# A graph layer: part of one gathered tile in every 11th group comes by identity products on TensorE, and the prologue is laid out anew

## The chip, the cores and the metric

The kernel runs on one core of a Trainium2 chip. Its time is the device time of one execution in microseconds. The kernel before takes 1875.99 us, the median of three runs (1874.75 to 1878.42). The trace shown here comes from one more execution, which took 1872.44 us and whose instructions span 1870.6 us.

The engines are named as the profile names them: PE is TensorE's products and PEld its weight loads, DVE is VectorE, ACT is ScalarE, POOL is GpSimd and SP is SyncE, which only issues transfers here.

## The reference

The layer has 12500 nodes with 64 features and 212500 edges with 32 features. The edges are sorted by destination. All numbers are f32.

```python
msg_in = jnp.concatenate([nodes[row], nodes[col], edge_features], axis=-1)
messages = relu(msg_in @ mW1 + mb1) @ mW2 + mb2
aggregated = jax.ops.segment_sum(messages, col, num_segments=nodes.shape[0])
upd_in = jnp.concatenate([nodes, aggregated], axis=-1)
out = relu(upd_in @ uW1 + ub1) @ uW2 + ub2
result = _layernorm(nodes + out, axis=-1)
```

`row` is the source of an edge and `col` its destination. The costly part is `nodes[row]`: 212500 rows of 64 features, read in no order.

## The kernel before

**Groups and steps.** The edges are cut into 554 groups of 384, each of three tiles of 128. Because the edges are sorted, the destinations of a group lie in a window of 32 nodes. One step of the main loop handles three groups at once on TensorE: it turns group k (`turn`, L372), forms the hidden layer of group k - 2 (`hidden`, L399) and sums group k - 4 into its window (`sums`, L425). Every step is one unbroken run of matmuls; its first instruction waits for all that the three parts need, and its last one releases what follows.

**Where source features come from.** For most tiles POOL issues an indirect transfer (`gather`, L164 to L175, issue at L167) that brings 128 rows into a slot of a ring of 20 groups. It works 16 groups ahead of the steps; the slot of group g is free when group g - 20 has been turned. TensorE then turns the rows into columns (L378, one product with an identity for each tile), so that features lie along the partitions, and ACT copies the result from PSUM to SBUF (L389). The first tile of the groups in `COPIED`, 181 of them, has no gather: the node features lie in SBUF as columns (`own_xc`, 64 partitions by 12500), and DVE and ACT copy one column of 4 bytes for each edge straight into its place (`fetch`, L553 to L569). Each step copies 44 columns: 20 on DVE (L565), 24 on ACT (L567). The addresses come from a table of sources (`src_copied`): SP loads a piece for eight steps, DVE turns it into addresses (L531), and before each part a register load on the copying engine brings up to 12 of them into registers (L546). From step 18 (`BEGIN`) to step 543 the steps copy columns; the last 10 (`SHORT`) do not.

**The other parts of a step.** DVE writes the one-hot of the destinations in the window (L366), which lies beside the gathered rows. The hidden layer is a product of 128 turned rows (64 features, 32 one-hot, 32 edge features) with 128x128 weights in which the 32 middle rows are the window's projected nodes (L404); DVE applies the relu (L415). The sums multiply the hidden layer as weights with the one-hot (L431). The one-hot is repeated `TIMES` = 4 times as the moving operand, which gives 128 columns of which 32 are used. Every fourth step counts the edges of each node (L442). Every 23 steps or so a chunk of 512 nodes is finished and updated (L474 to L516).

**The prologue.** SP loads tables and the eight weight tiles (L217, L218). ACT fills the sums with zeros (L267) and the ones row of `own_xc` and the zeros beside it (L206, in a small and a large piece). The projections of the nodes by their destination weights (`projected`, L335) go through two buffers to a table in DRAM (L343, L344), from which the windows are read (L358). At step 8 the checks on the edges' order and the combined weights are made (L281 to L310).

## Time and profile before

| what | value |
|---|---|
| median of three runs | 1875.99 us |
| the profiled execution | 1872.44 us |
| its span | 1870.6 us |
| busy: PE, PEld | 1302.0 us, 1139.3 us |
| busy: DVE, ACT, POOL | 1452.9 us, 1558.7 us, 1400.1 us |
| mean granted TensorE clock | 0.952 |

Busy times of PE and PEld overlap each other, and a product's end is modelled; the distance between the starts of two instructions says more of their cost than their durations. A row of a group gives, behind its name, the shapes, the count, the busy time in us, the mean duration in ns, and the idle time of the engine just before, with what ended it. For TensorE the shape is `128*96 128x128`: rows and columns of the weights, then partitions and columns of the operand that moves (in a weight load's row, the weights again). In a row of the timeline the first two numbers are the start and the time covered, and `x6` says that six neighbours of one kind were put together. A row of stretches gives their bounds, their length, then the busy time and count of PE, PEld, DVE, ACT and POOL, the granted clock as a share, the share of the DMA engines and GB/s.

### The profile page before, as it was taken

The page shows a single profiled execution, that of the slowest core. Times are in us where ns is not written, and L with a number is a line of the kernel's source. Part 1 is how long each engine was busy: PE and PEld are TensorE (multiplying, and loading weights), DVE is VectorE, ACT ScalarE, POOL GpSimd, SP SyncE. Part 2 cuts the span into 40 slices and gives each one's busy share as a digit, 9 for nine tenths or more (in the row PEclk, how much of TensorE's full clock was granted, in tenths as well). Part 3 has the DMA queues.
Part 4 walks back from the last instruction along what each step waited for, and adds up shares of the span by engine and source line. Part 5 has one row for each costly group of instructions (what it writes and reads, how often), then busy time and mean ns, then how long its engine had stood idle before and what let it go on. Part 6 is the DMA issues. An engine that isn't in the chain of part 4 may idle for free. (4 is left out here: it accounts for less than half of the span.)

```text
span 1870.6 us, 55967 instructions
## 1 busy us (share of the span) xinstructions
PE 1302.0 (70%) x9839; PEld 1139.3 (61%) x9839; DVE 1452.9 (78%) x13141; ACT 1558.7 (83%) x13374; POOL 1400.1 (75%) x1488
## 2 busy tenths in 40 slices
PE   1777777677767667677676776776767767667676
PEld 0676666666666556566665666665656656556665
DVE  1338888899897888877887878888878888888773
ACT  5249999999998888888888888888888888888871
POOL 7777777777777777777777777777777777777774
PEclk9889999999999998998999998999998999999999
DMA  4543222222222222222222222222222222222221
GB/s 93 138 123 75 54 54 54 51 54 53 52 54 48 50 52 49 50 49 45 54 52 47 52 46 54 48 51 48 53 46 53 45 54 51 48 53 48 50 49 26
DMA packets 112796, 104.10 MB, mean 56 GB/s; under 512 B 51586, under 2 KB 82960, under 8 KB 112432
## 3 DMA queue, kind: packets, MB, share of 16 engines
q0 software_dynamic: 47392, 48.60, 14.8%
q1 hardware_dynamic: 64196, 51.35, 10.0%
q14 instruction: 280, 2.29, 0.4%
q8 instruction: 84, 1.38, 0.3%
q10 hardware_dynamic: 844, 0.48, 0.1%
HBM read 90.61 MB, written 9.62 MB: 54 GB/s over the span
## 5 line engine op out<-in xcount | busy, mean ns | idle before, releaser
L167 POOL DMA_INDIRECT own_s<-in_x,src_sb x1481 | 1399.4, 945 | 452.5 <-issue 342.9
L567 ACT ACTIVATE own_st<-own_xc 64x4 uint8 x12560 | 1265.6, 192 | 60.2 <-issue 52.2
L565 DVE COPY own_st<-own_xc 64x4 uint8 x10480 | 884.5, 190 | 17.3 <-issue 9.2
L378 PE MATMUL own_ps<-own_ident,own_s 128*96 128x128 f32 x1661 | 294.1, 288 | 488.7 <-DMA own_s<-in_x,src_sb 164.0
L378 PEld LDWEIGHTS own_ps<-own_ident,own_s 128*96 128x96 f32 x1661 | 169.1, 131 | 593.5 <-issue 291.0
L431 PE MATMUL own_ps<-own_s,own_h 128*128 128x128 f32 x3322 | 490.3, 287 | 1.2 <-DVE own_h L415 0.6
L404 PE MATMUL own_ps<-own_wm,own_st 128*128 128x128 f32 x3322 | 485.5, 285 | 0.0
L415 DVE TENSOR_SCALAR own_h<-own_ps 128x384 f32<-128x384 f32 x553 | 302.1, 547 | 185.5 <-PE own_ps L442 84.7
L431 PEld LDWEIGHTS own_ps<-own_s,own_h 128*128 128x128 f32 x3322 | 443.3, 203 | 2.3 <-DVE own_h L415 1.2
L404 PEld LDWEIGHTS own_ps<-own_wm,own_st 128*128 128x128 f32 x3322 | 437.8, 201 | 1.8 <-issue 1.2
L389 ACT ACTIVATE own_st<-own_ps 96x384 f32<-96x384 f32 (+2 forms) x734 | 294.2, 401 | 167.5 <-PE own_ps L442 81.6
L458 DVE TENSOR_TENSOR own_agg<-own_ps,own_agg 128x32 f32 x554 | 105.8, 191 | 170.6 <-DVE own_h L415 90.4
L366 DVE TENSOR_TENSOR own_s<-iota,dlc 128x96 f32<-128x96 f32 x554 | 136.2, 247 | 0.3 <-issue 0.2
L442 PE MATMUL own_ps<-own_s,own_one 128*1 128x128 f32 x834 | 120.6, 283 | 0.0
L463 DVE TENSOR_TENSOR own_xc<-own_ps,own_xc 1x32 f32 x554 | 101.9, 184 | 18.5 <-DVE own_xc L463 1.8
L442 PEld LDWEIGHTS own_ps<-own_s,own_one 128*1 128x1 f32 x834 | 60.2, 85 | 35.7 <-issue 3.6
L340 PE MATMUL u_ps<-w1b,own_xc 65*128 65x128 f32 x196 | 33.4, 323 | 58.1 <-ACT t L343 38.8
L340 PEld LDWEIGHTS u_ps<-w1b,own_xc 65*128 65x128 f32 x196 | 29.1, 227 | 62.3 <-ACT t L343 42.1
L343 ACT ACTIVATE t<-u_ps 128x512 f32<-128x512 f32 (+1 forms) x25 | 14.7, 588 | 58.2 <-DMA by_dst<-t 37.9
L487 PE MATMUL u_ps<-same,own_xc 65*128 65x64 f32 (+1 forms) x196 | 37.0, 271 | 1.5 <-ACT u L480 1.4
L489 PE MATMUL u_ps<-u,u 128*128 128x64 f32 (+1 forms) x196 | 38.0, 276 | 0.0
L487 PEld LDWEIGHTS u_ps<-same,own_xc 65*128 65x128 f32 (+1 forms) x196 | 29.7, 191 | 2.3 <-ACT u L480 2.2
(62 smaller groups left out, 257.1 us busy)
## 6 DMA issues: line engine op xcount, KB each, us to landing
own_st<-in_efT SPq DMA_DIRECT2D x138, 192.0 KB
own_s<-in_x,src_sb POOLq DMA_INDIRECT x1481
own_wm<-by_dst SPq DMA_DIRECT2D x554, 16.0 KB
by_dst<-t SPq DMA_DIRECT2D x24, 256.0 KB
out<-o SPq DMA_DIRECT2D x24, 128.0 KB
own_xc<-in_xT SPq DMA_DIRECT2D x12, 179.2 KB
index<-in_src_copied SPq DMA_DIRECT2D x65, 1.4 KB
dlc_i<-in_dst_cols SPq DMA_DIRECT2D x1, 831.0 KB
```

The lines of the kernel that those rows point to most:

```text
L167: nc.gpsimd.indirect_dma_start(out=s[:p, j, :D], out_offset=None, in_=x[:, :], in_offset=bass.IndirectOffsetOnAxis(ap=src_sb[:p, g * TG + ...
L366: places_by[g] = nc.vector.tensor_tensor(own.s[g % RING][:, :, D:], iota.unsqueeze(1).to_broadcast([P, TG, W]), dlc[:, g * TG : (g + 1) * ...
L378: nc.tensor.transpose(xt[:, j * P : j * P + p], s[:p, j, :], ident[:p, :p])
L389: after(nc.scalar.activation(t[r, c : c + n][:, m], xt[r, m], AF.Copy), step))
L404: nc.tensor.matmul(pre[:p, j, :], t[:, c + j * P : c + j * P + p], wm[g % NW], start=True, stop=True)
L415: relu_by[g] = [nc.vector.tensor_scalar(h, pre, 0.0, None, ALU.max)]
L431: did.append(nc.tensor.matmul(sg, h[:p, j, :], s[:p, j, D:].unsqueeze(1).to_broadcast([p, TIMES, W]), start=j == 0, stop=j == len(sizes) - 1))
L442: did.append(nc.tensor.matmul(at_ps[:, : len(whole)], own.one, own.ring[:, first_s : first_s + len(whole), j, D:], start=j == 0, stop=j == ...
L458: did = [after(nc.vector.tensor_tensor(agg[:, at], sg[:, 0, :], agg[:, at], ALU.add), step)]
L463: did.append(after(nc.vector.tensor_tensor(count, counted, count, ALU.add), step))
L565: by[engine] = nc.vector.tensor_copy(o, x_at)
L567: by[engine] = nc.scalar.activation(o, x_at, AF.Copy)
```

## The change

It has two parts.

**Products instead of gathers.** In 47 groups (29, 40, and so on to 535, `BY_PE`) the third tile loses its gather. Its 128 source columns are brought by TensorE: behind the matmuls of each step, `side_fetch` issues up to 12 matmuls with the same weights, the first 64 rows and 96 columns of the identity, and one moving column each, a column of `own_xc` at an address from a register. The result goes straight to the place in PSUM where the turned tile would stand; rows 64 to 95 come out as zeros. The 128 columns take 11 steps. In front of each step's matmuls `side_columns` loads the step's addresses into TensorE's registers. In the step that turns such a group, the third tile's turning is replaced by a product of its one-hot with the identity, which fills rows 64 to 95. The table of sources has 56 entries for each step instead of 44. The one-hot of the sums is repeated twice instead of four times (`TIMES`).

**The prologue.** The zeros of the sums are written by DVE in 16 pieces, two ahead of the first projections and one in each of the first 14 steps. The ones row and the zeros below it, now with the row of counts, are written by ACT in a piece for each of the first 16 steps, behind the early piece. Half of the weight tiles' loads, most of the destination table, and the update weights go behind the first windows. The projections' rows have four buffers instead of two.

```diff
-TIMES = 4
+TIMES = 2
+PCOLS = 12
+PERIOD = 11
+EACH = COLS + PCOLS
+SIDE = 512 - P
+BY_PE = [g for g in range(BEGIN + PERIOD, G - SHORT, PERIOD)]
...
-            for j, p in enumerate(tiles_of(g)) if j or g not in columned
+            for j, p in enumerate(tiles_of(g))
+            if (j or g not in columned) and (j < TG - 1 or g not in by_pe)
...
-    rowp = ctx.enter_context(tc.tile_pool(name="rows", bufs=2))
+    rowp = ctx.enter_context(tc.tile_pool(name="rows", bufs=4))
...
-    nc.scalar.activation(agg.rearrange("p (a b) -> p a b", a=P),
-                         zero.unsqueeze(1).to_broadcast([P, P, NP // P]), AF.Copy)
-    rest(NEAR_NODES, NP)
...
         nc.sync.dma_start(xc[:D, slice(*nodes)], a["xT"][:, slice(*nodes)])
+        rest(nodes[0], nodes[1] if k < BITS - 1 else NP)
+
+    def zeroed(k):
+
+        n0, n1 = (NP * i // BITS for i in (k, k + 1))
+        nc.vector.memset(agg[:, n0:n1], 0.0)
...
+        xt = ps[0][: D + W, 512 - GE :] if g in by_pe else ps[0][: D + W, :GE]
+        did = []
+        for j, p in enumerate(tiles_of(g)):
+            cols = slice(j * P, j * P + p)
+            if j == TG - 1 and g in by_pe:
+                did.append(nc.tensor.matmul(xt[D:, cols], s[:, j, D:], ident,
+                                            start=True, stop=True))
+            else:
+                did.append(nc.tensor.transpose(xt[:, cols], s[:p, j, :], ident[:p, :p]))
...
+    def side_columns(k):
+
+        if k < BEGIN:
+            return None
+        n, m = divmod(k - BEGIN, PERIOD)
+        c0, c1 = m * PCOLS, min(P, (m + 1) * PCOLS)
+        if n >= len(BY_PE) or c0 >= c1:
+            return None
+        return BY_PE[n], c0, loaded(k, COLS, c1 - c0, ET.PE)
+
+    def side_fetch(k, work):
+
+        if work is None:
+            return
+        g, c0, v = work
+        for c, at in enumerate(v, SIDE + c0):
+            i = nc.tensor.matmul(own.ps[g % 2][0][: D + W, c : c + 1], ident[:D, : D + W],
+                                 xc_bytes[:D, bass.ds(at - own.at, 4)].bitcast(F32),
+                                 start=True, stop=True)
+            tc.no_tile_sem_insts.add(i.ins.name)
+            tc.add_to_no_dep_group("quiet", i.ins)
+            kept[:] = [i.ins]
...
-    inputs(0)
-    inputs(1)
     for g in range(LEAD):
         onehot(g)
+    placed()
     places(0)
+    weights(SB)
+    inputs(0)
+    for i in (0, 1):
+        zeroed(i)
     projected(0)
     projected(1)
     for g in range(SB):
         window(g)
+    nc.sync.dma_start(dlc_i[:, near:], a["dst_cols"][:, near:])
+    update_weights()
+    weights(NW)
+    inputs(1)
+    relative(NEAR_GROUPS, G)
...
+            side = side_columns(k)
             between.append(lambda: registers(k, 0))
             step((turn, k), *([(hidden, k - 2)] if k > 1 else []),
                  *([(sums, k - 4)] if k > 3 else []))
+            side_fetch(k, side)
```

More of the change, by code (lines that the diff above doesn't have):

```diff
@@ L44 @@
 NEAR_NODES = 1024
+NEAR_GROUPS = 16
 BITS = 16
@@ L139, in ordered @@
     efs_by, hidden_by, counted_by = {}, {}, {}
-    columned = set(COPIED)
+    columned, by_pe = set(COPIED), set(BY_PE)
     def after(first, *others):
-        tc.declare_no_dep(first.ins, group="quiet", reason="waits for the last of a step")
+        keep = kept if first.ins.engine == ET.PE else []
+        tc.declare_no_dep(first.ins, group="quiet", keep=keep,
+                          reason="waits for the last of a step")
         for i in others:
@@ L189, in ordered @@
     nc.vector.memset(eps, EPS)
-    zero = const.tile([P, NP // P], F32, name="zero")
-    nc.vector.memset(zero, 0.0)
     nc.vector.tensor_copy(ident, ident_t)
@@ L544, in registers @@
                 return
[L545 to L551 removed]
+            held[part] = engine, c0, loaded(k, offset, count, engine)
     def fetch(*parts):
```

116 lines of the change are left out of this document (65 added, 51 removed).

## The prediction

> **What bounds the kernel now.** I read the page first (busy shares, slices, groups), then POOL's waits, then three stretches with TensorE's counts, and last TensorE's timeline, because the change moves work from POOL to TensorE.
>
> ```profile
> span 1870.6 us, 55967 instructions
> PE 1302.0 (70%) x9839; PEld 1139.3 (61%) x9839; DVE 1452.9 (78%) x13141; ACT 1558.7 (83%) x13374; POOL 1400.1 (75%) x1488
> L167 POOL DMA_INDIRECT own_s<-in_x,src_sb x1481 | 1399.4, 945 | 452.5 <-issue 342.9
> L567 ACT ACTIVATE own_st<-own_xc 64x4 uint8 x12560 | 1265.6, 192 | 60.2 <-issue 52.2
> ```
> ```profile
> L167 POOL DMA_INDIRECT own_s<-in_x,src_sb x1481: 901/944/1667, 3.0 to 1852.5; - x186
> ```
> ```profile
> POOL own_s L167 <- issue: 342.9, 1125, 0.3
> POOL own_s L167 <- DMA own_s<-in_x,src_sb: 85.3, 280, 0.3
> POOL own_s L167 <- PE own_ps L431: 19.2, 63, 0.3
> ```
>
> By busy share ACT (83%) looks like the bound and POOL (75%) does not. POOL's waits say otherwise: the idle time in front of a gather is never longer than 0.3 us (last column), whoever is named as its releaser. The gathers run from 3.0 to 1852.5 us, so one takes (1852.5 - 3.0) / 1480 = 1.2497 us, 0.945 busy and 0.30 of issue, and POOL stands still for nothing else. POOL bounds the whole span: 1481 gathers in a row, then 18 us for the last groups.
>
> ```profile
> 0.00:121.69 121.69, 61.67 (x412) 56.98 (x413) 32.71 (x126) 41.61 (x40) 90.84 (x102) 0.90 0.50 120
> 121.69:1792.75 1671.06, 1187.78 (x9035) 1038.14 (x9034) 1379.88 (x12736) 1488.63 (x13127) 1263.23 (x1339) 0.96 0.24 52
> 1792.75:1870.60 77.85, 52.59 (x394) 44.20 (x394) 40.36 (x281) 28.48 (x209) 46.06 (x49) 0.93 0.19 39
> ```
> ```profile
> 121.69:1792.75 1671.06, 273.07 (x1551) 155.50 (x1551) 0.96 0.24 52
> ```
>
> The columns are PE, PEld, DVE, ACT, POOL, then the granted clock. The middle stretch runs from step 18 to step 534; the row in the second fence counts only its turning (L378), three per step, so it holds 1551 / 3 = 517 steps of 3.23 us. These are the 517 steps that the change gives new TensorE work. In front of it TensorE is late: the gathers of group 18 are issued by 3.0 + 57 x 1.25 = 74 us, its step runs at 121.7.
>
> **What a pass on TensorE costs.** A matmul in f32 is two passes, each a weight load and a product; a turning is one. Busy times overlap here, so I go by starts in the timeline.
>
> ```profile
> 86.91 0.97 PEld L340 LDWEIGHTS u_ps<-w1b,own_xc 65*128 65x128 f32 x8
> 87.80 0.35 PEld L378 LDWEIGHTS own_ps<-own_ident,own_s 128*96 128x96 f32 x3
> 88.13 0.75 PEld L404 LDWEIGHTS own_ps<-own_wm,own_st 128*128 128x128 f32 x6
> 88.80 0.75 PEld L431 LDWEIGHTS own_ps<-own_s,own_h 128*128 128x128 f32 x6
> 89.47 0.97 PEld L340 LDWEIGHTS u_ps<-w1b,own_xc 65*128 65x128 f32 x8
> ```
> ```profile
> 802.95 1.02 PE L474 MATMUL u_ps<-own_agg,wc 128*128 128x512 f32 x2
> 803.81 1.02 PE L475 MATMUL u_ps<-own_xc,ux 97*128 97x512 f32 x2
> 809.40 0.39 PE L489 MATMUL u_ps<-u,u 128*128 128x64 f32 x2
> 809.63 0.39 PE L487 MATMUL u_ps<-same,own_xc 65*128 65x64 f32 x2
> 809.85 0.39 PE L489 MATMUL u_ps<-u,u 128*128 128x64 f32 x2
> ```
> ```profile
> 1859.51 0.20 PEld L442 LDWEIGHTS own_ps<-own_s,own_one 128*1 128x1 f32 x6
> 1859.65 0.26 PEld L448 LDWEIGHTS own_ps<-own_s,own_one 128*1 128x1 f32 x4
> 1862.07 0.27 PEld L489 LDWEIGHTS u_ps<-u,u 128*106 128x106 f32 x2
> 1862.25 0.35 PEld L487 LDWEIGHTS u_ps<-same,own_xc 65*106 65x106 f32 x2
> ```
> ```profile
> L306 PE MATMUL u_ps<-valid,ones x4: 163/164/164, 78.1 to 80.0; 128*1 128x1 f32 x4
> L442 PEld LDWEIGHTS own_ps<-own_s,own_one 128*1 128x1 f32 x834 | 60.2, 85 | 35.7 <-issue 3.6
> 1003.45 0.28 PEld L378 LDWEIGHTS own_ps<-own_ident,own_s 128*96 128x96 f32 x3 [1.76 <-ACT own_st L567]
> ```
>
> With 128 weight columns and 128 moving columns six passes take 0.67 us, 0.112 each (88.13 to 88.80). With 64 moving columns a pass still takes 0.111 (809.40 to 809.85, four passes): the weight load sets it. With 512 moving columns it is 0.43 (802.95 to 803.81, two), and the weight load vanishes in it. With 106 weight columns it is 0.09 (1862.07 to 1862.25, two); with one weight column and 32 moving ones 0.02 to 0.03 (1859.51 to 1859.65, six). So a pass lasts as long as the longer of its weight load and its product, and the load goes by its columns, about 0.85 to 0.88 ns for each. L306 has four records for two matmuls with one moving column: two passes there too. L442 uses one and the same weights in every matmul and yet loads them every time (834 loads, as many as its products on the page's list).
>
> **The change, part by part.** *Gathers.* The 47 groups lose one gather each: 47 x 1.2497 = 58.7 us of POOL's row. That is the whole gain if POOL stays the bound: 1870.6 - 58.7 = 1811.9.
>
> *Column products.* 47 tiles of 128 columns are 6016 matmuls, two passes each: 12032 passes, 24 in a full step. Each loads the 64x96 identity for a single moving column. No such pass is in the trace. From above: 0.09 us (106 columns). From below: 0.03 (one column). I take 96 / 128 x 0.112 = 0.084, next to the 106 column row, since the load goes by columns. That is 12032 x 0.084 = 1011 us, 2.0 us in a full step. TensorE has not that much room. Its own passes in the middle stretch are 9034 x 0.112 = 1012, and 92 of them, the 512 column ones of 23 chunks, cost 0.32 more: 29; together 1041. The room is 1671 - 1041 = 630 us, against 1011.
>
> *The third tile's one-hot* in those 47 groups becomes a product of two passes with 128 moving columns instead of one turning: about 0.11 x 47 = 5 us.
>
> *Register loads on TensorE*, one of up to 12 values per step:
>
> ```profile
> L546 ACTq TENSOR_LOAD <-index x1047: 549/782/1358, 123.6 to 1814.8; - x175
> ```
>
> On ACT one takes 0.78 us in the sequencer. On TensorE it is queued behind the 24 passes of the step before, and the whole step that follows is queued behind it. I take nothing for it, covered by those 2.0 us of passes already issued; uncovered it is 517 x 0.782 = 404 us.
>
> *TIMES 4 to 2* halves the moving columns of the sums to 64. By the 809 rows a pass stays at 0.111: nothing, and no loss.
>
> *Prologue.*
>
> ```profile
> L343 ACT ACTIVATE t<-u_ps 128x512 f32<-128x512 f32 (+1 forms) x25 | 14.7, 588 | 58.2 <-DMA by_dst<-t 37.9 <-PE u_ps L340 16.0 <-PE own_ps L431 4.3
> L206 ACT ACTIVATE own_xc<-own_ident 32x1024 f32<-32x1024 f32 (+1 forms) x2 | 10.8, 5424 | 0.0
> L267 ACT ACTIVATE own_agg<-zero 128x12544 f32<-128x12544 f32 x1 | 10.7, 10657 | 9.9 <-DMA own_wm<-in_mW 9.9
> L191 DVE MEMSET zero<- 128x98 f32 x1 | 0.1, 140 | 0.0
> 10.86 0.54 SPq L217 DMA_DIRECT2D own_wm<-in_mW  x1
> 22.08 0.88 SPq L316 DMA_DIRECT2D own_st<-in_efT  x2
> ```
>
> Two fills leave ACT's queue ahead of the first table copy: 10.7 + 9.8 = 20.5 us. The zeros come back on DVE as 16 pieces of 784 columns, at most 8 x 0.14 = 1.1 us each, 18 us, in a stretch where DVE works 32.7 of 121.7 us; the ones come back on ACT in 16 pieces of about 0.8 us, where it works 41.6. On SP half of the 16 weight loads (10.86 to 22.08) go behind the first features. The seven update weights on ACT's queue and the larger part of the destination table on SP go behind the first windows; they are first used at steps 8 and 10, so I take nothing. Nothing new stands ahead of POOL's gathers. Four row buffers instead of two can take some of the 37.9 us for which the copies wait for their own writes; I count 13. While POOL is the bound all this is worth nothing, since POOL starts at 3.0 either way. Once TensorE is, it counts: step 18 moves from 121.7 to 121.7 - 20.5 - 13 = 88, between 77 (its gathers) and 122 (no help).
>
> *Tail.* 77.9 us are now 49 gathers long. With POOL up to 20 groups ahead I estimate 70, between 58 and 78.
>
> *Sum.* 88 + (1041 + 5 + 1011 = 2057) + 70 = 2215 us of span, 2217 with the 1.8 that the profiled execution (1872.44) has around its span; the median of the runs shown, 1875.99, is 0.2% above that execution: 2220. A middle step becomes 2057 / 517 = 3.98 us instead of 3.23, and POOL, with 1434 gathers, waits for the ring. ACT and DVE, 1488.6 and 1379.9 us busy in those 1671, keep their work and get slack.
>
> **The rivals.** *A, POOL stays the bound: faster.* One mechanism: the identity's load costs next to nothing. For it: the three 96 column loads of a turning (1003.45) stand in 0.28 us all told, and a one column weight pass costs 0.03. Against it: those rows turn data in one pass or load a single column; 106 columns of plain f32 took 0.09. It decides at (1671 + 34 + 8 - 1046) / 12032 = 0.055 us per pass; at or under (1671 - 59 - 1046) / 12032 = 0.047 the time is 1811.9 + 1.8, with the 0.2% 1817. [...] *A', in between:* a pass midway between 0.03 and 0.09 gives 2220 - 12032 x 0.024 = 1931.
>
> *B, loads and products do not overlap, or the register load is exposed.* A pass of 0.084 + 0.028 adds 337 us: 2557; an uncovered register load adds 404: 2624. For it: no product here has so short a stream to hide a load in, and no register load stands in TensorE's queue now. Against it: the 512 column rows swallow their loads whole. [...]
>
> *C, the clock falls, or register-addressed products run at ACT's pace.*
>
> ```profile
> 60.00:80.00 20.00, 8.00 (x60) 6.28 (x59) 7.21 (x22) 2.54 (x5) 15.10 (x16) 0.76 0.57 140
> 1500.00:1520.00 20.00, 12.52 (x102) 10.93 (x102) 15.52 (x142) 16.37 (x146) 15.15 (x16) 1.00 0.28 58
> ```
>
> The granted clock was 0.76 where PE worked 8 of 20 us, 1.00 with 12.5 of 20. One-column products may count as little work: 0.76 instead of 0.96 in the middle makes 2057 into 2598, the time 2760. ACT's register-addressed copies take 1265.6 / 12560 = 0.101; in series with the load a pass is 0.185: 3435.
>
> *D, the change does not relieve POOL* cannot be: the gathers leave the list.
>
> **Chances and range.** TensorE bound at 0.080 to 0.092 a pass 0.64, its own range 2150 to 2360; A 0.11; A' 0.03 (0.01 of it within 0.2%); B 0.16; C 0.06. The range, 2060 to 2750, reaches from below TensorE's own range to over both prices of B and leaves out A, A' and C, 0.20. A measurement can tell about 0.2%: faster 0.11, same 0.01, slower 0.88.
>
> **What would show it.** Right: POOL with 1434 gathers and idle times of many us that TensorE's turning ends; PE and PEld each with about 21,900 records; column passes 0.08 to 0.09 us apart; steps of about 4.0 us in the middle; ACT's share well under 83%; the first turning before 37.9 us. Wrong: gathers still 1.25 us apart (A), passes 0.11 or more apart or gaps of 0.8 us at each step's head (B), a granted clock under 0.9 in the middle (C).

## The result, and the profile after

The changed kernel takes 3932.02 us, the median of four runs (3911.54 to 3978.18); the kernel before took 1875.78 us beside it (1874.75 to 1878.42). The ratio is 2.092, with a 95% interval of 2.083 to 2.101; it leaves out the longest of the four runs, which showed a lower clock (0.589) than the others (0.597 to 0.599). The forecast said slower, and named TensorE as the new bound; both came true. Its time, 2220 us, and its range, 2060 to 2750 us, did not. The profiled execution took 3926.39 us.

These are lines of the page after: the span, the engines' busy time, the granted clock in 40 slices and the costliest groups. In the changed kernel a gather is L177, a column product L625, a turning L413, ACT's copy of the turned tiles L422, a hidden product L437 and a sum L464.

```profile
span 3924.6 us, 86426 instructions
PE 3688.3 (94%) x21918; PEld 3436.5 (88%) x21918; DVE 1497.3 (38%) x13158; ACT 1634.9 (42%) x13388; POOL 1359.9 (35%) x1441
PEclk8556565665665655565555555665655555555567
L177 POOL DMA_INDIRECT own_s<-in_x,src_sb x1434 | 1359.1, 948 | 2483.0 <-PE own_ps L464 1438.3
L625 PEld LDWEIGHTS own_ps<-own_xc,own_ident 64*96 64x96 f32 x12032 | 1665.2, 238 | 263.6 <-ACT own_st L422 192.1
L625 PE MATMUL own_ps<-own_xc,own_ident 64*96 x12032 | 1709.3, 271 | 140.7 <-ACT own_st L422 137.5
L437 PE MATMUL own_ps<-own_wm,own_st 128*128 128x128 f32 x3322 | 754.4, 392 | 0.0
```

The kernel before had these two rows for the clock and for the hidden products:

```profile
PEclk9889999999999998998999998999998999999999
L404 PE MATMUL own_ps<-own_wm,own_st 128*128 128x128 f32 x3322 | 485.5, 285 | 0.0
```

POOL has its 1434 gathers and now waits 2483 us, mostly for TensorE (1438.3 us for its sums, 731.3 for its counts). TensorE is busy 94% of the span. But the clock row is new: it read 8 or 9 in every slice before, and reads 5 or 6 in all but the first and the last here. The hidden products carry no change at all in the diff and their records grew from 285 ns to 392 ns. The same three stages as in the forecast, with the columns PE, PEld, DVE, ACT, POOL and the clock:

```profile
0.00:89.00 89.00, 57.62 (x412) 53.42 (x412) 43.88 (x143) 34.31 (x54) 66.53 (x75) 0.92 0.54 141
89.00:3851.90 3762.90, 3575.95 (x21112) 3337.26 (x21112) 1416.64 (x12768) 1574.74 (x13150) 1293.37 (x1367) 0.58 0.10 24
3851.90:3924.60 72.70, 54.71 (x396) 45.77 (x395) 36.81 (x249) 25.87 (x186) 0.00 (x0) 0.88 0.05 14
```

The prologue (89 us) and the tail (72.7) are where the forecast put them (88 and 70). Everything that is missing is in the middle: 3763 us in place of 2057, with a clock of 0.58. The timeline of TensorE shows the same step twice, once at full clock (492.14) and once at half (497.39); the first number is the start, the second the time covered.

```profile
492.14 2.19 PE L625 MATMUL own_ps<-own_xc,own_ident 64*96 x24
494.27 0.53 PE L413 MATMUL own_ps<-own_ident,own_s 128*96 128x128 f32 x3
494.63 0.83 PE L437 MATMUL own_ps<-own_wm,own_st 128*128 128x128 f32 x6
...
497.39 4.00 PE L625 MATMUL own_ps<-own_xc,own_ident 64*96 x24 [0.75 <-ACT own_st L422]
501.31 0.88 PE L413 MATMUL own_ps<-own_ident,own_s 128*96 128x128 f32 x3
501.98 1.49 PE L437 MATMUL own_ps<-own_wm,own_st 128*128 128x128 f32 x6
503.26 1.38 PE L464 MATMUL own_ps<-own_s,own_h 128*128 128x64 f32 x6
```

At full clock 24 column passes take 494.27 - 492.14 = 2.13 us. The starts inside such a run are 0.085 us apart (median of some 3800), so the 0.084 of the forecast was right. At half clock they are 0.160 apart (median of some 7700), and a 128 column pass takes 0.213 in place of 0.112.

In both traces the granted clock has two values only, 1.0 and 0.5 (82 records before, 288 after), and its changes lie whole multiples of 3.413 us apart. The records of half clock add up to 181 us before and 3168 us after. A window is, from here on, a stretch of that length on the grid of these changes. What goes with the clock shows in consecutive windows of after: first all products that overlap them (the count in brackets), then the column products alone; the clock is the column behind.

```profile
485.12:488.53 3.41, 3.24 (x16) 0.50 0.00 1
488.53:491.95 3.42, 3.42 (x33) 1.00 0.09 18
491.95:495.36 3.41, 3.41 (x37) 1.00 0.33 88
495.36:498.77 3.41, 2.66 (x16) 0.50 0.16 38
498.77:502.19 3.42, 3.42 (x21) 0.50 0.06 16
```
```profile
485.12:488.53 3.41, 0.01 (x1) 0.50 0.00 1
488.53:491.95 3.42, 1.51 (x16) 1.00 0.09 18
491.95:495.36 3.41, 2.19 (x24) 1.00 0.33 88
495.36:498.77 3.41, 1.38 (x9) 0.50 0.16 38
498.77:502.19 3.42, 2.62 (x17) 0.50 0.06 16
```

The window at 491.95 is busy from end to end with 37 products, and the next one is at half clock; the one at 485.12 holds only 16, and the next one is at full clock. The difference is in the second fence: 24 of the 37 are column products, only 1 of the 16 is. Counted over the whole traces, by the starts of a step's own passes in each window (turning, hidden, sums, counts and update; a pass of 512 columns as four, a column product as none), this is the share of windows that are followed by one at full clock, with the number of windows:

| own passes in the window | under 11 | 11 or 12 | 13 or 14 | 15 to 17 | 18 and more |
|---|---|---|---|---|---|
| before | 0 (24) | 0.27 (30) | 0.87 (38) | 1.00 (160) | 0.99 (280) |
| after | 0 (628) | 0.07 (116) | 0.20 (162) | 0.68 (188) | 0.98 (46) |
| after with `TIMES = 4` | 0 (556) | 0.29 (150) | 0.87 (132) | 0.93 (176) | 0.95 (39) |

So a window with 13 or 14 own passes was followed by full clock just as often (0.87) before, where there are no column products, as after with `TIMES = 4`, where a full step has 24 of their passes; with fewer than 11 own passes none was. With `TIMES = 2` a third of the own passes stream 64 columns, and 13 or 14 gave 0.20, 15 to 17 gave 0.68. This also shows why the clock comes back so seldom. A step has some 18 own passes. At full clock its 24 column passes take 2.1 us of a window, which leaves room for some 12 own ones. At half clock they take 24 x 0.160 = 3.84 us, more than a whole window, and a window without any of them has room for 3.41 / 0.213 = 16 own passes.

### The profile page after: what moved, and what is told of

Its sections match the earlier page's. It is cut to its first block, busy times and chain, and to the rows that moved or that the text cites. A ratio compares the mean times of both kernels' runs of the same rounds, so it can differ in the third digit from the quotient of the medians.

```text
span 3924.6 us, 86426 instructions
## 1 busy us (share of the span) xinstructions
PE 3688.3 (94%) x21918; PEld 3436.5 (88%) x21918; DVE 1497.3 (38%) x13158; ACT 1634.9 (42%) x13388; POOL 1359.9 (35%) x1441
## 4 chain that ended last, share of the span: by engine, by line
issue 45%; PE 27%; POOL 23%; DMA 2%; ACT 1%; DVE 0%; SPq 0%; ACTq 0%; POOLq 0%; DVEq 0%
POOL own_s L177 23%; PE own_ps L625 12%; PE own_ps L437 5%; PE own_ps L464 5%; PE own_ps L413 3%; PE own_ps L475 1%; DMA own_s<-in_x,src_sb 1%; ACT own_st L422 1%; PE u_ps L369 1%; PE u_ps L520 0%; PE u_ps L522 0%; ACT own_st L605 0%; PE u_ps L507 0%; DMA by_dst<-t 0%; DMA own_xc<-in_xT 0%
## 5 line engine op out<-in xcount | busy, mean ns | idle before, releaser
L177 POOL DMA_INDIRECT own_s<-in_x,src_sb x1434 | 1359.1, 948 | 2483.0 <-PE own_ps L464 1438.3
L625 PEld LDWEIGHTS own_ps<-own_xc,own_ident 64*96 64x96 f32 x12032 | 1665.2, 238 | 263.6 <-ACT own_st L422 192.1
L625 PE MATMUL own_ps<-own_xc,own_ident 64*96 x12032 | 1709.3, 271 | 140.7 <-ACT own_st L422 137.5
L422 ACT ACTIVATE own_st<-own_ps 96x384 f32<-96x384 f32 (+2 forms) x734 | 298.7, 407 | 2041.8 <-PE own_ps L464 1308.1
L437 PE MATMUL own_ps<-own_wm,own_st 128*128 128x128 f32 x3322 | 754.4, 392 | 0.0
L464 PEld LDWEIGHTS own_ps<-own_s,own_h 128*128 128x128 f32 x3322 | 718.2, 311 | 6.3 <-DVE own_h L448 4.7
L464 PE MATMUL own_ps<-own_s,own_h 128*128 128x64 f32 x3322 | 716.0, 383 | 4.1 <-DVE own_h L448 3.1
L437 PEld LDWEIGHTS own_ps<-own_wm,own_st 128*128 128x128 f32 x3322 | 695.7, 302 | 19.8 <-issue 15.7
L413 PE MATMUL own_ps<-own_ident,own_s 128*96 128x128 f32 x1614 | 426.6, 393 | 53.1 <-DMA own_s<-in_x,src_sb 26.5
L413 PEld LDWEIGHTS own_ps<-own_ident,own_s 128*96 128x96 f32 x1614 | 216.0, 169 | 69.3 <-issue 35.8
L475 PE MATMUL own_ps<-own_s,own_one 128*1 128x128 f32 x834 | 174.1, 369 | 0.0
```

What stands on the lines that cost most here:

```text
L177: nc.gpsimd.indirect_dma_start(out=s[:p, j, :D], out_offset=None, in_=x[:, :], in_offset=bass.IndirectOffsetOnAxis(ap=src_sb[:p, g * TG + ...
L413: did.append(nc.tensor.transpose(xt[:, cols], s[:p, j, :], ident[:p, :p]))
L422: after(nc.scalar.activation(t[r, c : c + n][:, m], xt[r, m], AF.Copy), step))
L437: nc.tensor.matmul(pre[:p, j, :], t[:, c + j * P : c + j * P + p], wm[g % NW], start=True, stop=True)
L464: did.append(nc.tensor.matmul(sg, h[:p, j, :], s[:p, j, D:].unsqueeze(1).to_broadcast([p, TIMES, W]), start=j == 0, stop=j == len(sizes) - 1))
L475: did.append(nc.tensor.matmul(at_ps[:, : len(whole)], own.one, own.ring[:, first_s : first_s + len(whole), j, D:], start=j == 0, stop=j == ...
```

## The experiments

On three of the chips used here the kernel before itself takes about 2435 us (last section); each run is set against the kernel before on its own chip.

The theory after the two traces was the one just told: one-column products do not count as work for the clock. Its rivals were the other parts of the change (narrow sums, prologue), the register loads that sit between the steps, and the wait of the products for ACT's copy.

**First: is it the clock, the prologue, or the narrower sums?** One chip, kernel before 2434.52 us.

```diff
 e1_times4
-TIMES = 2
+TIMES = 4
```

> The changed kernel with TIMES back at 4 and nothing else. Where the granted clock was 0.5 for 3168 of 3925 us, the theories differ in what lowers it. Theory S (a stretch of products with one moving column streams almost nothing through the array, so the clock is cut): the sums' six passes stream 0.107 instead of 0.053 us each, which helps a little; mean clock 0.62 to 0.75, time 3100 to 3800. Theory T (the sums' halved moving columns lower it): clock over 0.9, time near 2340, which is 3925 less half of the 3168 us at half clock. Theory G (gaps in front of each step, from the register load on TensorE, lower it): as measured, about 3930.

3700.39 us in one run, clock 0.68. The wide sums bring some windows back (third row of the table), not most of them.

```diff
 e2_no_products
-BY_PE = [g for g in range(BEGIN + PERIOD, G - SHORT, PERIOD)]
+BY_PE = []
...
```

> The changed kernel without the column products: all 181 + 47 groups' third tiles are gathered as before, 1481 gathers; the new prologue and TIMES = 2 stay. Theories S and G: clock near 0.95 as in the kernel before, POOL bounds, and the time is that of before within 0.3% (1872 to 1880), since the prologue lies beside POOL's row. Theory T: the sums' passes at half the stream lower the clock under 0.8; a step's 15 passes at half clock take about 3.2 us, so TensorE becomes a second bound and the time goes over 1950.

2458.11 us, a ratio of 1.009 (1.005 to 1.012). Without the products the loss is gone but for a remainder; the times that were expected (1872 to 1880) were for a chip on which the kernel before takes 1876. The next run says where the remainder may be from.

```diff
 e4_before_times2 (the kernel before)
-TIMES = 4
+TIMES = 2
```

> The kernel before with TIMES = 2 and nothing else. Theories S and G: POOL bounds as before; the array streams about 1.45 instead of 1.77 us of a 3.23 us step, the clock may fall a little below 0.95, the time is within 0.5% of before (1868 to 1885). Theory T: clock under 0.8 and time over 1950.

2446.58 us, 1.006 (1.003 to 1.009), clock 0.773 where the kernel before has about 0.84 on these chips. Narrow sums by themselves cost about half a per cent there, with a lower clock beside it.

```diff
 e3_wide64: each column product streams its column up to 64 times
-            i = nc.tensor.matmul(own.ps[g % 2][0][: D + W, c : c + 1], ident[:D, : D + W],
-                                 xc_bytes[:D, bass.ds(at - own.at, 4)].bitcast(F32),
-                                 start=True, stop=True)
+            n = min(64, 512 - c)
+            x_at = xc_bytes[:D, bass.ds(at - own.at, 4)].bitcast(F32)
+            i = nc.tensor.matmul(own.ps[g % 2][0][: D + W, c : c + n], ident[:D, : D + W],
+                                 x_at.to_broadcast([D, n]), start=True, stop=True)
```

> The changed kernel, but each column product streams its one column up to 64 times into the places that the following products write anyway (later products overwrite them, so the result is the same). A pass with 64 moving columns streams 0.053 us and stays bound by its weight load of about 0.085. Theory S: the array now streams for over half of every stretch, clock over 0.9, column passes at 0.085, time 2250 to 2400. Theories T and G: clock near 0.6 and time near 3930 as before the edit.

3972.48 us, clock 0.628: a miss. The places end at column 512 (`min(64, 512 - c)`), so the last 63 of a tile's 128 columns get fewer than 64. A pass still takes 0.085 us, and a window at full clock now holds its clock more often (windows with 11 or 12 own passes: 0.93 of 40, against 0.19 of 42 after). But at half clock, where most windows are, it changes nothing: of such windows 0 of 85 brought the clock back, against 0 of 75 after.

**Second: how many products are too many, and does more dense work bring the clock back?** One chip, before 2437.94 us. The first three have `TIMES = 4`.

```diff
 e5_pcols4 (15 groups)            e7_pcols8 (30 groups)
-PCOLS = 12                       -PCOLS = 12
-PERIOD = 11                      -PERIOD = 11
+PCOLS = 4                        +PCOLS = 8
+PERIOD = 33                      +PERIOD = 17
```

> The changed kernel with TIMES = 4, 4 columns in a step instead of 12, for 15 groups instead of 47 (every 33rd). 8 passes of 0.085 are 0.68 us, less than the 1.2 us that TensorE idles in a step of the kernel before. Window theory (the clock of the next 3.41 us is full only where about 11 or more of the 128 column passes fell into the last 3.41 us, and column products count nothing): the products take idle time, a window holds as many counted passes as before, so the clock stays within 0.05 of the kernel before's; where POOL bounds, the time falls by 15 x 1.25 = 19 us, 1%. If every column product lowers the clock whatever else fills the time: clock down by a third of the loss seen with 12, and 10% or more slower.

> The changed kernel with TIMES = 4, 8 columns in a step and 30 groups (every 17th). 16 passes are 1.36 us, a little more than the idle time. Window theory: between the kernel before and the one with 12: a step of 3.4 to 3.6 us at full clock holds about 15 counted passes per window, enough; but once at half clock a step takes 6 us and holds 9, not enough. Clock 0.7 to 0.9, time 2000 to 3000. By work alone, without the clock: 3.4 / 3.23, 5% above before.

Four: 2733.58 us, 1.121 (1.113 to 1.128), clock 0.802. Eight: 3197.67 us in one run, clock 0.731. Twelve had given 3700 on the chip of the first four runs. The loss grows with the number of products. That four still cost 12% was a miss: TensorE has room for eight more passes, so something beside their own time was at work.

```diff
 e6_extra_work: behind every third column product
+            if (c - SIDE - c0) % 3 == 2:
+                i = nc.tensor.matmul(
+                    own.ps[k % 2][2][:, 256:].rearrange("p (t w) -> p t w", w=P), ident,
+                    ident.unsqueeze(1).to_broadcast([P, 2, P]), start=True, stop=True)
...
```

> The changed kernel with TIMES = 4 and, behind every third column product, one more f32 matmul of the identity with itself, 128 weight columns and 256 moving ones, into unused places of PSUM: four in a full step, 8 passes of 0.215 us, 1.7 us of pure extra work at full clock. Window theory: every stretch of 3.41 us now holds the equivalent of 13 or more counted passes, so the clock rises to over 0.85 and the kernel becomes faster than the one with TIMES = 4 alone (3700) though it does more: about 3000 to 3400. If the clock falls with the load or with the count of weight loads: clock not above 0.68, and time 3700 plus 517 x 1.7 / 0.68 = 5000.

6171.91 us, clock 0.644: a miss, and it tells little of the theory. The added passes of 256 columns take 0.588 us each at half clock; a round of six column passes and two such takes 2.2 us, so a window holds three of the added passes, worth six of 128 columns, and the work added is long in itself.

```diff
 e8_fixed_columns (the columns are then not those of the edges' sources)
-        return BY_PE[n], c0, loaded(k, COLS, c1 - c0, ET.PE)
+        return BY_PE[n], c0, range(c0, c1)
...
-                                 xc_bytes[:D, bass.ds(at - own.at, 4)].bitcast(F32),
+                                 xc[:D, at : at + 1],
```

> The changed kernel (TIMES = 2, 12 columns), but the column products read fixed columns instead of those that the table names, so TensorE loads no registers; the source features of those 47 tiles are wrong. Window theory: the same passes, the same clock, 0.58 to 0.64, and the time within 6% of the changed kernel's 3930. Gap theory (the register loads and address sums of TensorE's sequencer leave gaps, and these lower the clock): clock over 0.8 and time under 2800.

4030.58 us in one run, clock 0.586. The changed kernel took 4076.35 us on another chip (below), where the kernel before takes as long as here. The turnings of the two, the changed kernel first; the number behind the second bar is TensorE's idle time in front of them:

```profile
L413 PE MATMUL own_ps<-own_ident,own_s 128*96 128x128 f32 x1614 | 433.2, 398 | 55.2 <-issue 25.4
L413 PE MATMUL own_ps<-own_ident,own_s 128*96 128x128 f32 x1614 | 422.3, 390 | 5.8 <-issue 3.4
```

Without the register loads 49 us of idle time at the head of the steps are gone, which fits the 46 us between the two times. So the loads cost about 1%, not the 404 us of rival B, and they do not lower the clock: it is 0.586 without them and 0.592 with them.

**Third: dense work between the products, and a bank that nobody reads.** One chip, before 2435.42 us. The changed kernel and the kernel before were run there as well.

> The changed kernel unchanged, beside the kernel before on this chip, where the kernel before takes longer than in the first comparison (2438 instead of 1876). TensorE bounds the changed kernel, so what slows the kernel before here should hardly touch it: 3900 to 4000, clock 0.58 to 0.63, ratio 1.6. If the same thing slows both: over 4500.

> The kernel before unchanged, for its profile on this chip. If TensorE's clock alone makes it 2438 here: ACT's copies run in one piece as in the first profile (60 us idle inside them) and the clock is well under 0.8. If the engines' instructions come late: hundreds of us of idle time inside the runs of copies on ACT and DVE with nothing that they wait for, as with TIMES = 2 (430 and 324 us), and the clock falls only as a result, to about 0.8 or more.

4076.35 us, 1.673 (1.669 to 1.677), and 2434.34 us.

```diff
 e9_dense_between (TIMES = 4): behind each column product
+            i = nc.tensor.matmul(own.ps[(k + 1) % 2][1][:, 512 - P :],
+                                 own.h[(k - 1) % NH][:, 0], own.h[(k - 1) % NH][:, 1],
+                                 start=True, stop=True)
...
```

> The changed kernel with TIMES = 4 and one more f32 product of hidden-layer values, 128 weight columns and 128 moving ones, behind each of the 12 column products, into unused places of PSUM: 24 passes of 0.112 us, 2.7 us of pure extra work in a full step, 1390 us over 517 steps. Window theory: at full clock no stretch of 3.41 us then holds fewer than about 14 counted passes, so the clock, once full, stays full: over 0.9, against 0.68 with TIMES = 4 alone; the time is 517 x 6.8 + 170 = 3700, no more than with TIMES = 4 alone (3700), with 1.4 ms of work more. Where column products lower the clock in any company, or load lowers it: clock 0.68 or less and time 3700 + 1390 / 0.68 = 5700.

7905.23 us, clock 0.639: a miss. A pass with 64x96 weights that follows one with 128x128 starts 0.205 us after it, and the next one 0.106 behind that; one with 128x128 that follows one with 64x96 starts 0.150 after it, and the next one 0.213 behind that (medians at full clock). Farther on in a run of one kind the distances are 0.085 and 0.112. So a round of two column passes and two dense ones takes 0.674 us, and a window at full clock holds ten dense passes: too few by the table, where none with fewer than 11 was followed by full clock.

```diff
 e12_free_bank (the source features of the 47 tiles are left out)
-            i = nc.tensor.matmul(own.ps[g % 2][0][: D + W, c : c + 1], ident[:D, : D + W],
+            i = nc.tensor.matmul(own.ps[(k + 1) % 2][1][: D + W, c : c + 1], ident[:D, : D + W],
...
+        nc.vector.memset(own.ps[i][0][:, SIDE:], 0.0)
```

> The changed kernel, but the column products go to places in a PSUM bank that no engine reads at that time (the other parity's hidden-layer bank), and the places where they belong are set to zero once; the source features of those 47 tiles are left out. If every second step's products wait for ACT's copy out of their own bank, 137 us of TensorE's idle time in front of them go: 3 to 6% under the changed kernel, more if the clock rises with it. If that idle time lies beside other waits: no change.

3823.87 us in one run, 252 us under the changed kernel on the same chip, at the same clock (0.594 and 0.592). The wait of the column products for ACT's copy is gone:

```profile
L625 PEld LDWEIGHTS own_ps<-own_xc,own_ident 64*96 64x96 f32 x12032 | 1705.6, 243 | 105.4 <-issue 63.5
L625 PE MATMUL own_ps<-own_xc,own_ident 64*96 x12032 | 1749.4, 275 | 0.0
```

The wait itself is visible in the groups after: 192.1 us ahead of the loads and 137.5 ahead of the products, which lie beside each other, named as ACT's copy L422. Group k is turned into bank k % 2, and the columns of group g go to bank g % 2, so in every second step the column products write the bank that ACT is about to read, and a semaphore holds the first of them until that copy is done. This is a cost of its own, but with twelve products the clock stays down without it too.

**Fourth: the same work in another order.** One chip, before 1873.28 us. Both have `TIMES = 4` and eight dense products in each step, beside the twelve column products; they differ in the place of the block alone.

```diff
 e13_block_middle                          e14_block_end
+  if c - SIDE - c0 == 5:                  +  if c - SIDE - c0 == len(v) - 1:
+      for _ in range(8):                  +      for _ in range(8):
+          i = nc.tensor.matmul(own.ps[(k + 1) % 2][1][:, 512 - P :],
+                               own.h[(k - 1) % NH][:, 0], own.h[(k - 1) % NH][:, 1],
+                               start=True, stop=True)
...
```

> The changed kernel with TIMES = 4 and, behind the 6th of the 12 column products of a step, 8 f32 products of hidden-layer values in a row (16 passes of 0.112, 128 weight columns, 128 moving), into unused places of PSUM. The first two tries to hold the clock up put their extra passes where changing between 64 and 128 weight rows cost 0.2 us each time, so their windows still held only about 10 counted passes. Here no window of 3.41 us at full clock can hold fewer than about 16: two stretches of column products of 1.2 us, 1.8 us of extra work between them, 1.9 us of the step's own. Window theory: clock over 0.9, a step of 6.1 us, time 3200 to 3500, less than with TIMES = 4 alone (3700) though each step has 1.8 us more to do. Load theory, or column products lowering the clock in any company: clock 0.7 or less and time 3700 + 517 x 1.8 / 0.68 = 5000 or more.

> The same instructions as in the run before it in this list, but the 8 extra products stand behind the last of a step's column products instead of behind the 6th, so that the column products keep one stretch of 2.1 to 2.4 us. Window theory: a window that covers this stretch holds at most 1.2 us of counted work, 10 or 11 passes, under the limit: the clock falls again, to 0.65 to 0.85, and the time is 3800 to 4800, clearly above the run with the same work split. If only the amount of work of each kind counts: both alike.

The clock rows and the groups of the added products, of the block in the middle and of the block at the end:

```profile
PEclk9999989999899999999999999999988899999999
L633 PE MATMUL own_ps<-own_h 128*128 128x128 f32 x8272 | 1103.9, 289 | 0.0
```
```profile
PEclk9888888988889988888898888888888888889888
L633 PE MATMUL own_ps<-own_h 128*128 128x128 f32 x8272 | 1393.5, 338 | 0.0
```

In the middle: 3699.38 us, clock 0.964. At the end: 3976.47 us, clock 0.865, just above the 0.65 to 0.85 that were expected. There is one run of each. The instructions are the same and the order alone makes 7.5%: the one that cuts the run of column products in two keeps the clock, as expected, though it has two changes to or from the 64x96 weights more in each step. So in these two runs the clock went down with one-column work that stands in one piece (0.865 against 0.964), and not with its total. With the block in the middle the time was above the 3200 to 3500 that were expected: a step takes 6.85 us instead of 6.1, since the changes of weights and the wait for ACT's copy (137.4 us ahead of the products) stay.

**Fifth: four products again, two, and none, on a chip where the kernel before takes 1873.34 us.** All have `TIMES = 4`.

```diff
 e15_pcols4_again           e16_pcols2 (8 groups)      e17_prologue_times4
-PCOLS = 12                 -PCOLS = 12                -BY_PE = [g for g in ...]
-PERIOD = 11                -PERIOD = 11               +BY_PE = []
+PCOLS = 4                  +PCOLS = 2
+PERIOD = 33                +PERIOD = 65
```

> The kernel with 4 columns in a step, 15 groups and TIMES = 4 once more, in case this chip is one on which the kernel before takes about 1875. There TensorE's products would lie in idle time while POOL bounds: with the clock as it was, 15 x 1.25 = 19 us faster, 1857, ratio 0.990. If they meet the wait for their own PSUM bank, which puts ACT's lateness into TensorE's row, or take the clock down: slower than before, ratio 1.01 to 1.15. Where the kernel before takes 2435: ratio 1.12 again.

> 2 columns in a step, 8 groups (every 65th), TIMES = 4. By the same two readings: 8 x 1.25 = 10 us faster, ratio 0.995, where POOL bounds and nothing else happens; half of what 4 columns lose, ratio 1.01 to 1.08, where the bank's wait or the clock decides.

> The new prologue alone: no column products, 1481 gathers, TIMES = 4. Where POOL bounds from 3 us on, the prologue is beside it: ratio 0.998 to 1.002. Where POOL does not bound, the 20 to 33 us that step 18 comes earlier could show: ratio 0.986 to 1.0. With TIMES = 2 it took 1.0089 of the kernel before, against 1.0058 for TIMES = 2 alone.

No products: 1874.94 us, 1.001 (1.0001 to 1.002): the new prologue is worth nothing while POOL is the bound. Four: 2246.62 us, 1.192 (1.184 to 1.200), clock 0.867. Two: 3118.31 us, 1.665 (1.662 to 1.667), clock 0.735, a clear miss, since fewer products cost more. Its register loads on ACT (rows of four products, then of two; the middle number is the median in ns) and what the column products waited for tell why it cannot be compared:

```profile
L570 ACTq TENSOR_LOAD <-index x1047: 548/781/1272, 92.6 to 2194.9; - x175
```
```profile
L570 ACTq TENSOR_LOAD <-index x1047: 778/1058/3174, 92.6 to 3046.1; - x175
  ACT own_st L422: 1693.4, 513
```

With two products the table of sources has 46 entries for each step, and the register loads on ACT, and on DVE (1356 in place of 843), became slow; ACT's copies came late, and the column products, which wait for one of them in every second step, waited 1693 us, counted once ahead of the loads and once ahead of the products, which lie beside each other. Whether the 46 entries are the reason was not tried.

**Last: four products without the wait.** On a chip where the kernel before takes 1872.37 us, four products for each step as above, written to a bank that nobody reads.

```diff
 e18_pcols4_free_bank, against e15_pcols4_again (the source features of the 15 tiles are left out)
-            i = nc.tensor.matmul(own.ps[g % 2][0][: D + W, c : c + 1], ident[:D, : D + W],
+            i = nc.tensor.matmul(own.ps[(k + 1) % 2][1][: D + W, c : c + 1], ident[:D, : D + W],
...
+        nc.vector.memset(own.ps[i][0][:, SIDE:], 0.0)
```

> Four column products per step, 15 groups, TIMES 4, as before, but the products go to a bank of PSUM that no engine reads while they run. (The source features of the third tile of these 15 groups are left out.) With the products in the tile's own place the time was 2246.6 us, 1.192 of the kernel before, the clock 0.867, and the products were idle for 226 us behind ACT's copy of the turned tiles, which reads the same bank in every second step. Theory bank: this wait is what four products cost: without it TensorE's windows stay full, the clock returns above 0.93, and POOL is the bound again: ratio 0.99 to 1.05, 1855 to 1965 us. Rival, the eight short passes and the register load in TensorE's queue thin out the work by themselves: the idle time behind ACT goes, but the clock stays under 0.90 and the ratio is 1.10 to 1.20, 2060 to 2250 us.

1853.99 us (1853.47 to 1854.84), 0.990 (0.988 to 0.992), clock 0.961. First four products in the tile's own bank, then in the free one: the engines, what the column products waited for, and POOL's longest wait (last number) for a sum.

```profile
PE 1878.1 (84%) x13694; PEld 1665.6 (74%) x13694; DVE 1481.6 (66%) x13158; ACT 1594.9 (71%) x13388; POOL 1389.0 (62%) x1473
  ACT own_st L422: 510.8, 444
POOL own_s L177 <- PE own_ps L464: 215.8, 179, 4.0
```
```profile
PE 1656.4 (89%) x13694; PEld 1488.9 (80%) x13694; DVE 1465.4 (79%) x13160; ACT 1550.7 (84%) x13388; POOL 1387.0 (75%) x1473
  issue: 48.8, 143
POOL own_s L177 <- PE own_ps L464: 10.7, 35, 0.3
```

(The 510.8 us count the wait twice, 284.7 ahead of the loads and 226.1 ahead of the products.) The passes are the same, 13694 with as many loads: without the wait the clock comes back, POOL waits no more than 0.3 us, and the time falls by 18.4 us under the kernel before, which is 15 gathers at 1.2497 (18.7). So at four products the wait, with the clock that it takes along, is the whole loss; the two runs are on two chips, on which the kernel before differs by 1 us. How it comes about is in the timeline of ACT and then of TensorE with four products in the tile's own bank:

```profile
1019.96 2.46 ACT L605 ACTIVATE own_st<-own_xc 64x4 uint8 x24 [0.38 <-issue]
1022.43 0.66 ACT L422 ACTIVATE own_st<-own_ps 32x128 f32<-32x128 f32 x2
```
```profile
1020.79 0.83 PE L464 MATMUL own_ps<-own_s,own_h 128*128 128x128 f32 x6
1023.14 0.88 PE L625 MATMUL own_ps<-own_xc,own_ident 64*96 x8 [1.52 <-ACT own_st L422]
```

ACT's copy of the turned tiles stands in ACT's queue behind the 24 column copies of the step, 2.46 us. TensorE ends its step at 1021.6 and then stands for 1.52 us, until ACT is through. For its own sake that copy is needed only two steps later, by the hidden products. The standing time empties windows too, and the clock falls on top of it: counted as in the table, 115 windows hold fewer than 11 own passes in this run, and 29 with the free bank.

A version that wins would have to put the columns in a bank of their own until their group is turned. It was not tried.

## Why the prediction was wrong

**What bounds the kernel** and **Gathers** were right. POOL kept 1434 of its 1481 gathers, and where nothing else happens (four products, free bank) each gather taken away gives back 1.23 us, as the forecast's 1.2497 said. POOL's idle times in front of a gather are ended by TensorE's sums and counts, not by the turning that the forecast named.

**Column products** was the step that failed, in one part: the price was right, the state was not. It took 0.084 us from rows at full clock and added 12032 of them, 1011 us, to a middle stretch whose other passes it left at 0.112. At full clock both are right, 0.085 and 0.112. But the products made the clock fall to half for 81% of the span, where they take 0.160 and 0.213, and a middle step takes 7.28 us instead of the 3.98 of the forecast. Rival C named the mechanism (one-column products may count as little work), but its quoted row shows another case, a TensorE that stands idle (0.76 of the clock with 8 of 20 us busy); here it was busy. It was also mis-sized: it took 0.76 for the whole middle, where 0.58 was measured, and it got a chance of 0.06, together with another case. The sum that was needed is that of own passes in 3.41 us: 18 in a step of 3.98 us are 15 on average, with a third of them narrow, and uneven, since 24 column passes stand in one piece. The windows that fall short then lengthen the step, which brings the average down too; the measured clock was 0.597.

How much of the loss is the clock can be estimated from the run with the block in the middle, whose clock is 0.964. Its mean step of 6.85 us holds the block: 0.150 us to the first dense pass, 0.213 to the second, 14 x 0.112 to the last, then 0.205 and 0.106 to the next two column passes, in place of two distances of 0.085. That is 2.07 us more. Without it the step is 4.78 us, 517 steps are 2471 us, and with 90 and 69 for the prologue and the tail of that run the span is some 2630. Against the forecast's 2215 that leaves some 410 us for what the clock does not do, and of 3924.6 some 1300 us for the clock. The two are not independent, since waits empty windows, and that run itself spends 270 us at half clock.

**What lies between** those numbers was not in the sum at all. One is the wait for the bank: 192 us ahead of the loads after, and the whole loss with four products. It follows from two lines of code that stood in the diff, the bank `g % 2` of the columns and the bank of the turning. In the trace the semaphore holds products that write other columns of the bank than ACT reads (0.75 us at 497.39). The other is the change to the 64x96 weights and back in every step. At full clock the first column pass starts 0.205 us after its forerunner in place of 0.112 and the second 0.106 in place of 0.085; the first turning starts 0.150 after the last column pass in place of 0.085, and the second 0.151 in place of 0.109. That is 0.22 us a step, 114 us. Within a run of dense products loads and products do overlap: a pass takes 0.111 us with 64 moving columns (the 809 rows) and 0.112 with 128, where 64 columns more are by themselves an estimated 0.054 (an eighth of the 0.43 of 512). An added cost shows at some changes of the weights: at the two above and, in the kernel before, from a sum (128x128) to a count (128x1), 0.205; none from a turning (128x96) to a hidden product (128x128), 0.109, or between the 65x128 and the 128x128 of an update, 0.112 (medians at full clock).

**The third tile's one-hot** is 94 passes, too few to show. **Register loads on TensorE** were put at nothing and cost about 50 us: in 60 of the 511 steps that turn behind column products the turning starts late, by up to 1.0 us. With fixed columns and no loads this idle time falls from 55.2 us to 5.8, and with the free bank, loads and all, to 7.7. This suggests that the loads show only where the wait for the bank has held up TensorE's queue first.

**TIMES 4 to 2** was wrong. The pass keeps its 0.112 us at full clock (median), as the forecast said, but it counts for less with the clock: 13 or 14 own passes in a window were followed by full clock in 0.20 of the cases, against 0.87 with four repeats, and the times are 3700.39 us with four repeats against 4076.35 with two, on two chips whose kernel before takes 2435 us.

**Prologue and tail** were right: 89 and 72.7 us against 88 and 70, the first turning at 11.7 us, and worth nothing by themselves (1.001).

```profile
L413 PE MATMUL own_ps<-own_ident,own_s x1614: 220/421/448, 11.7 to 3908.8; 128*96 128x128 f32 x180
```

**Rivals A and A'** fell by the 0.085 us between column passes, each a product of one column that loads its own weights; **B** fell but for the changes of weights and some 50 us of register loads.

## What to carry to other kernels

When an edit gives TensorE many products with few moving columns, do not only add up their passes: count, for each 3.41 us of the new step, the passes of 128 moving columns, since here a window of that length was followed by one at half clock in about 0.7 of the cases when it held 11 or 12 of them (0.73 before, 0.71 after with `TIMES = 4`) and always when it held fewer, for the old work too. When new products write PSUM, list which engine reads the same bank in the same step and what is queued in front of that read: one wait of that kind, such as the 1.52 us shown, in every second step cost 393 us here (2246.62 against 1853.99), while the 3840 passes that waited cost nothing by themselves. And when a run with less of the change still loses, look for a wait that does not grow with it.

## What the runs showed that was not expected

- One-column products did not hold the clock here: no window with fewer than 11 own passes was followed by one at full clock (0 of 628 after), in a kernel whose TensorE was busy 94% of the span.
- Half clock held itself here: with 24 column passes a step needs 3.84 us for them at half clock (24 x 0.160), longer than a window, and of the windows at half clock with 11 or 12 own passes 0 of 75 brought the clock back.
- Register loads of 46 entries for each step had a median of 1058 ns on ACT and up to 3174, against 781 and 1272 with 48. The reason stays open.
- On three chips the kernel before took about 2435 us. Its trace there shows ACT's column copies with 193 ns each (192 in the first profile), but 462.1 us of idle time in front of them (60.2 there), of which 450.3 end with no event, and POOL no longer the bound:

```profile
L167 POOL DMA_INDIRECT own_s<-in_x,src_sb x1481 | 1398.2, 944 | 961.1 <-issue 340.4 <-remote 263.3 <-PE own_ps L431 171.7
L567 ACT ACTIVATE own_st<-own_xc 64x4 uint8 x12560 | 1357.6, 193 | 462.1 <-issue 450.3 <-DMA by_dst<-t 0.7
```

Why instructions come late on those chips was not settled.
